# A second pair of heads' keys by seven products: context sums made earlier, weight pieces on POOL, nine warming products

## The chip, the cores and the metric

The kernel runs on one core of a Trainium2 chip. The metric is device time in microseconds (us) for one execution. A core has a matrix engine (PE; its weight loads are listed as PEld), a vector engine (DVE), a scalar engine (ACT), a general engine (POOL) and a queue engine (SP) that issues the DMA transfers here. Each runs its own list of instructions in order, and semaphores make one engine wait for another. Matmuls write to PSUM, a memory of eight banks; everything else lies in SBUF.

## What is computed

The reference is a gated cross-attention block followed by a gated feed-forward block. What matters here is the product of the context with the key weights, for 32 batches of 64 tokens (2048 tokens), 32 heads of 128, and a model width of 512:

```python
def _L0_xattn_ref(hidden_q, hidden_kv, attention_mask, position_bias, Wq, Wk, Wv, Wo):
    B, S, D, H, DH = (2, 128, 512, 32, 128)
    ...
    q = (hidden_q @ Wq).reshape(b, lq, h, dh)
    k = (hidden_kv @ Wk).reshape(b, lk, h, dh)
    v = (hidden_kv @ Wv).reshape(b, lk, h, dh)
    score = jnp.einsum('bqhd,bkhd->bhqk', q, k) * scale + position_bias
    ...
    return ctx @ Wo
...
x = x + jnp.tanh(g_xattn[0]) * _L0_xattn_ref(_layernorm(x, axis=-1), ctx_4096, mask_BxSxS2_bk0, fside_Bx32xSxS2_0, L0_xattn_Wq, L0_xattn_Wk, L0_xattn_Wv, L0_xattn_Wo)
x = x + jnp.tanh(g_ffn[0]) * _L0_ffn_ref(_layernorm(x, axis=-1), ...)
```

## The kernel before

**Stages.** The 2048 tokens are worked in two halves of 1024 (p = 0 and 1), the 32 heads in 16 pairs (n = 0 to 15). Each half makes the keys of all pairs (`stage_a`), then the values, then queries, scores, softmax and the output projection; the feed-forward block ends the program. Keys go to DRAM (`kd`) and come back later.

**Split numbers.** Matmuls are done on float32r values. To keep accuracy, each operand is split into a high half (an ACT cast to float32r, L90 or L296) and a low half (raw minus high, a subtraction on DVE or POOL, L91 or L300). One block product is three matmuls, high by high, high by low and low by high, for each of two pieces of 128 rows of the width: six matmuls, called passes here, of 128x128 by 128x512, all recorded at L100 in `mm3`.

**Blocks.** A pair's key product is seen as a product of 2 by 2 blocks. The context has b11, b21 (from the tile `f0`, the first 512 tokens), b12 and b22 (from `f1`); the pair's weights have a11, a12, a21, a22, each 128x256. It can be made in two ways:

- Plainly, by eight block products (`plain_half`, 48 passes), from the split blocks themselves. PSUM tiles are `ppk`, evicted by ACT at L400.
- By seven block products p1 to p7 (`unit`, 42 passes), from sums of blocks on both sides. `unit` makes p1, p6, p7, p5 and p2 and leaves p4 and p3 to a function `end`, which the next unit calls (`carry`) after its own p1. p2 is added into p1's PSUM tile `px`, p4 into p7's tile `pv`, p3 into p5's tile `pz`; so p2 waits until ACT has read `px` (L362), and p4 and p3 until DVE has added `pv` and `pz` to the result (L357).

For the seven products the context side needs p1 = b11, p2 = b21 and p3 = b22 and four sums (`sum_blocks`, L162): b12 - b11 (for p5, written over b11), `t2`, which is b22 minus that one (p6, tile `c0t` in the profile), b22 - b12 (p7, written over b12) and b21 - t2 (p4, written over b21). Each is two pieces of 128x512, subtracted and split on DVE, with casts on ACT. These are made once for a half and serve all pairs. On the weight side every pair has its own four sums s1 to s4 (L289, tile `wsk`) and seven splits (L296 on ACT, L300 on POOL, tiles `wk<pair>p<product>`).

**The first half's start.** `first_load` brings the weights of pair 0 and `f0`, then `f1`. While these come, 10 matmuls of the identity by itself keep PE busy (L520, tile `warm`; each shows as two passes). `first_blocks` then splits b11 (p1), b21 (p2), b12 (a plain block, `c0b`) and b22 (p3) as they land, makes the first matmuls of pair 0 directly from unsplit numbers (`very_first`, L408), and splits the four weight blocks of pair 1 with DVE (`prep_plain` with `weng`, which is `nc.vector`; tile `wk1a`), after which the raw weights of pair 3 are fetched into the buffer of pair 1's. Pairs 0 and 1 of this half are made plainly, and all later ones by seven products. In the second half all are made by seven products.

**What sets the order.** The order is written out by hand. Generators are put on the list `streams`, and each call of `beat` lets every generator go one step; the plain products have 8 beats a pair, a unit has 7. `sum_blocks` is a stream from pair 0 on (its last step is drained before pair 2). `key_blocks` is the stream of weight pieces on POOL and ACT: its loop over pairs takes seven steps a pair, in which it makes pair n's sums and pieces for p7, p6, p5 and p2, the p1 piece of pair n + 1, and the p4 and p3 pieces of pair n - 1; after the last of these it fetches the raw weights of pair n + 1 on SP. `wbp` has nine buffers for weight pieces, `kqp` two for finished keys, PSUM eight.

Of the kernel before, what the change touches and what calls it, by code (L numbers as in the profile page):

```python
# [43 lines left out]
def flamingo_block(ctx: ExitStack, tc: tile.TileContext, x, xT, ctxT, bias, mask, gx, gf,  # L44
# [17 lines left out]
    streams = []  # L62
# [93 lines left out]
    def sum_blocks(f, tags, nm, eng, out):  # L156
        b11, b21, b12, b22 = parts(f)
        t2 = [rows.tile([P, 512], F32, tag="row", name=f"{nm}t2_{kt}") for kt in range(2)]

        def sub(o, a, b):  # L160
            for kt in range(2):
                eng.tensor_tensor(o[kt], a[kt], b[kt], ALU.subtract)  # L162

        sub(b11, b12, b11)
        yield
        sub(b12, b22, b12)
        yield
        sub(t2, b22, b11)
        yield
        out["p6"] = act_block("p6", t2, tags, nm, eng)  # L170
        yield
        out["p7"] = act_block("p7", b12, tags, nm, eng)
        yield
        out["p5"] = act_block("p5", b11, tags, nm, eng)
        yield
        sub(b21, b21, t2)
        yield
        out["p4"] = act_block("p4", b21, tags, nm, eng)
# [79 lines left out]
    raw_of, wt = {}, {}  # L258
# [60 lines left out]
    def prep_plain(n, eng, only=None):  # L319
        raw = raw_of[("k", n)]  # L320
        out = wt.setdefault(("k", n), {})
        for i, a in enumerate(("a11", "a12", "a21", "a22")):
            if only is None or a in only:
                t = wbp.tile([P, 2, 256], F32R, tag="wb", name=f"wk{n}{a}")
                split(raw[:, i * 256:(i + 1) * 256], t[:, 0], t[:, 1], eng)
                out[a] = [(t[:, 0, kt * P:(kt + 1) * P], t[:, 1, kt * P:(kt + 1) * P]) for kt in range(2)]
# [104 lines left out]
    def first_blocks(p, f, tags, nm, weng, out, plain):  # L431
        g = p * NPR
        b11, b21, b12, b22 = parts(f)

        def block(q, raw, eng=nc.vector):
            t = big(tags[ORDER.index(q)], [P, 2, 2, 512], F32R, f"{nm}{q}")
            out[q] = []
            for kt in range(2):
                split(raw[kt], t[:, 0, kt], t[:, 1, kt], eng)
                out[q].append((t[:, 0, kt], t[:, 1, kt]))  # L440
                yield

        prep_plain(g, nc.gpsimd, ("a21",))
        yield from block("p1", b11, weng)
        prep_plain(g, nc.gpsimd, ("a22",))
        yield from block("p2", b21, weng)
        prep_plain(g, nc.gpsimd, ("a11", "a12"))
        plain.update({(1, 1): out["p1"], (2, 1): out["p2"]})
        plain["ps"] = very_first(raw_of.pop(("k", g)), wt["k", g], plain)
        yield  # L450
        fetch("k", g + 2, "r0")
        yield
        b12t = [rwp.tile([P, 2, 512], F32R, tag=f"r{2 + i}", name=f"{nm}b12{i}") for i in range(2)]
        plain[1, 2] = []
        for kt in range(2):
            split(b12[kt], b12t[0][:, kt], b12t[1][:, kt], nc.vector)
            plain[1, 2].append((b12t[0][:, kt], b12t[1][:, kt]))
            yield
        yield from block("p3", b22)
        plain[2, 2] = out["p3"]  # L460
        for a in ("a11", "a21", "a12", "a22"):
            prep_plain(g + 1, weng, (a,))
            yield
        raw_of.pop(("k", g + 1))
        fetch("k", g + 3, "r1")


    def next_blocks(f, tags, nm, out, gate):
# [47 lines left out]
    for _ in load_ctx(0, f, KT):  # L516
        pass
    warm = psum("warm")
    for i in range(10):
        nc.tensor.matmul(warm[:, :P], ident, ident, start=True, stop=True)  # L520
    fetch("k", 1, "r1")
    first = {}, {}
# [184 lines left out]
    def stage_a(p, first, fc, res, rot, more, enter, blocks):  # L707
        xc, plain = first
        f = None
        for n in range(NPR):  # L710
            g = p * NPR + n
            if n == 0 and plain:
                sums = sum_blocks(fc, res, f"c{p}", nc.vector, xc)
                streams.append(sums)
            if n == 0 and not plain:
                drain(blocks)
            if n == (1 if plain else 0):
                streams.append(key_blocks(p, n + 1))
            if n == 3:
                f = [big(f"f{j}", [P, KT, 512], F32, f"xf{p}_{j}") for j in range(2)]  # L720
                t7 = big(rot[7], [P, 2, 1024], F32, f"wvr{p}_0a")
                t8 = big(rot[8], [P, 2, 1024], F32, f"wvr{p}_0b")
                fetch_v(p, 0, [t7[:, 0], t7[:, 1], t8[:, 0], t8[:, 1]])
                if more:
                    more = paced(more, 2)
                    streams.append(more)
                xstat = x_stats(p)
                streams.append(xstat)
            if n == 5:
                vsum = [None] + [rwp.tile([P, 1024], F32, tag=f"r{2 + i}", name=f"vs{p}_0_{i}") for i in range(2)] + [None]  # L730
                v0 = paced(blocks_v(p, 0, rot, vsum, nc.vector, K_ORDER), 3)
                streams.append(v0)
            if 6 <= n < 6 + KT:
                for j in range(NCH):
                    nc.sync.dma_start(out=f[j][:, n - 6, :], in_=xT[p * NCH + j, n - 6])
            if n == 6 and p:
                drain(more)
                streams.append(acc_rstd(p - 1))
            if n == 10:
                drain(xstat)  # L740
                x_spread(p)
            if n == 10 and p:
                turned_acc = acc_turned(p - 1)
                streams.append(turned_acc)
            kt = k_tile(g)
            w = wt[("k", g)]

            def store(kt=kt, n=n):
                for i in range(2):
                    nc.sync.dma_start(out=kd[p][n][:, i, :], in_=kt[:, i, :])  # L750
            if n < 2 and plain:
                for j in range(2):
                    plain_half(w, plain, k_dst(kt), f"k{g}", j, plain["ps"] if n == 0 and j == 0 else None)
                store()
            else:
                if n == 2 and plain:
                    drain(sums)
                carry[:] = [unit(w, xc, None, k_dst(kt), f"k{g}", tuple(carry)), store]
        drain(v0)
        if p:  # L760
            drain(turned_acc)
        xnorm = paced(x_norm(p, f), 2)
        streams.append(xnorm)
        xq = {}
        for g in range(NG):
            if g == 2:
                drain(xnorm)
                streams.append(mask_stream(p))
                if p == 0:
                    streams.append(adapt)  # L770
            if g == NG - 1:
                t4 = pieces(rwp.tile([P, 1024], F32, tag="r1", name=f"x{p}t4"))
                fetch("q", p * NPR, "r0")
                bias = enter()
                streams.append(turned_blocks(f, [rot[(7 * NG + i) % 9] for i in range(7)], f"x{p}", nc.gpsimd, keep,
                                             t4, xq, bias, enter))
            for t in range(4):
                if t == 1:
                    if g + 1 < NG:
                        raw = [rwp.tile([P, 1024], F32, tag=f"r{i}", name=f"wvr{p}_{g + 1}_{i}") for i in range(4)]  # L780
                        fetch_v(p, g + 1, raw)
                        streams.append(blocks_v(p, g + 1, rot, None, nc.gpsimd, V_ORDER))
                    if g == NG - 2:
                        keep = {}
                        streams.append(turned_sums(f, f"x{p}", nc.gpsimd, keep))
                if t == 2 and g == NG - 1:
                    streams.append(prep("q", p * NPR, nc.gpsimd))
                vt = kqp.tile([P, 4, 512], F32, tag="kq", name=f"vt{p}_{g}_{t}")
                dst = {(i, j): vt[:, i * 2 + j, :] for i in range(2) for j in range(2)}
                after = unit(wt["v", p, g], xc, slice(t * P, (t + 1) * P), dst, f"v{p}_{g}_{t}", tuple(carry))  # L790

                def store(vt=vt, g=g, t=t):
                    for i in range(2):
                        for j in range(2):
                            nc.sync.dma_start(out=vd[p][2 * g + i][:, j * 4 + t, :], in_=vt[:, i * 2 + j, :])
                carry[:] = [after, store]
        enter()
        return xq
# [541 lines left out]
    for p in range(NPH):  # L1340
        qt = [rot[(7 * NG + i) % 9] for i in range(7)]
        rest = [t for t in rot if t not in qt]
        g = (p + 1) * NPR
# [118 lines left out]
```

## Time and profile before

| | us |
|---|---|
| three runs | 1519.61, 1519.88, 1520.21 |
| median | 1519.88 |
| profiled execution | 1520.39 |
| its span, first to last instruction | 1518.6 |
| granted TensorE clock, mean | 1.000 |

In the timeline a line has the start and the length in us, the engine, the source line, the operation, the tile written and those read, the shape, the number of instructions merged into the line, and in brackets the idle time ahead of them and what ended it. `c` is raw context, `c0p` a split context block or sum for a product, `c0b` the split plain block b12, `c0t` the sum t2, `rawk` raw key weights. Pair 0's plain products run from 5.77 to 17.55 us, pair 1's from 17.55 to 28.43, and pair 2's unit begins there. Most lines are short, so the table of costliest groups on the page has none of the first 30 us; the timeline of these has to be asked for by itself.

| stretch, us | DVE busy | ACT busy | POOL busy |
|---|---|---|---|
| 12 to 24.3 | 12.13 | 8.12 | 0.00 |
| 30 to 60 | 14.77 | 12.21 | 26.12 |

### The profile page before, as it was taken

The page shows a single profiled execution, that of the slowest core. Times are in us where ns is not written, and L with a number is a line of the kernel's source. Part 1 is how long each engine was busy: PE and PEld are TensorE (multiplying, and loading weights), DVE is VectorE, ACT ScalarE, POOL GpSimd, SP SyncE. Part 2 cuts the span into 40 slices and gives each one's busy share as a digit, 9 for nine tenths or more (in the row PEclk, how much of TensorE's full clock was granted, in tenths as well). Part 3 has the DMA queues.
Part 4 walks back from the last instruction along what each step waited for, and adds up shares of the span by engine and source line. Part 5 has one row for each costly group of instructions (what it writes and reads, how often), then busy time and mean ns, then how long its engine had stood idle before and what let it go on. Part 6 is the DMA issues. An engine that isn't in the chain of part 4 may idle for free.

```text
span 1518.6 us, 25096 instructions
## 1 busy us (share of the span) xinstructions
PE 1513.4 (100%) x8956; PEld 1278.3 (84%) x8956; DVE 941.6 (62%) x1587; ACT 717.7 (47%) x1582; POOL 1051.1 (69%) x1160
## 2 busy tenths in 40 slices
PE   9999999999999999999999999999999999999998
PEld 7888888888888888888888888888888888888887
DVE  5665554376677576666388755437666757666664
ACT  5444133355654664576344423335565466456511
POOL 4899378978675757668789947897867565766410
PEclk9999999999999999999999999999999999999999
DMA  5754554385335263442485664438533526444421
GB/s 206 279 195 153 188 178 167 138 280 186 129 132 184 89 221 140 149 144 76 159 290 204 235 208 176 167 138 287 179 131 128 186 90 219 143 154 132 112 70 70
DMA packets 130271, 254.79 MB, mean 168 GB/s; under 512 B 27393, under 2 KB 61185, under 8 KB 126050
## 3 DMA queue, kind: packets, MB, share of 16 engines
q1 hardware_dynamic: 129858, 252.67, 48.1%
q8 instruction: 70, 1.15, 0.3%
q10 hardware_dynamic: 288, 0.52, 0.1%
q14 instruction: 55, 0.45, 0.1%
HBM read 177.64 MB, written 75.51 MB: 167 GB/s over the span
## 4 chain that ended last, share of the span: by engine, by line
PE 100%; POOL 0%; DVE 0%; DVEq 0%; issue 0%; POOLq 0%
PE pa L100 23%; PE po L1015 8%; PE pxq L100 6%; PE pvq L100 6%; PE pzv L100 6%; PE pvv L100 6%; PE pxv L100 6%; PE pzq L100 6%; PE pzk L100 5%; PE pvk L100 5%; PE pxk L100 5%; PE ps L868 4%; PE pf L100 3%; PE pyq L100 3%; PE pyv L100 3%; PE pyk L100 3%
## 5 line engine op out<-in xcount | busy, mean ns | idle before, releaser
L100 PE MATMUL pa<-wo,ch 128*128 128x512 f32 x896 | 278.1, 391 | 0.0
L903 ACT COPY pt<-tp 32x256 f32<-32x256 f32 x452 | 182.4, 404 | 60.1 <-DVE tp L906 49.6
L100 PEld LDWEIGHTS pa<-wo,ch 128*128 128x128 f32 x896 | 166.8, 188 | 34.9
L100 PE MATMUL pa<-wo,cl 128*128 128x512 f32 x448 | 174.5, 390 | 0.0
L1064 DVE TENSOR_TENSOR acc<-pa,acc 128x512 f32<-128x512 f32 x192 | 129.9, 682 | 55.7 <-PE pa L100 55.7
L821 POOL TENSOR_TENSOR sm<-sm,madd 128x512 f32<-128x512 f32 x60 | 77.0, 1292 | 88.5 <-DMA sm<-bias 88.5
L895 POOL TENSOR_TENSOR sm<-sm,r 128x512 f32<-128x512 f32 x64 | 66.8, 1044 | 74.7 <-DVE r L894 74.0
L1015 PEld LDWEIGHTS po<-pt,v 128*128 128x128 f32 x960 | 111.6, 192 | 2.2
L1015 PE MATMUL po<-pt,v 128*128 128x128 f32 x960 | 112.5, 275 | 0.0
L873 POOL TENSOR_TENSOR sm<-sm,mx 128x512 f32<-128x512 f32 x64 | 67.0, 1048 | 62.1 <-DVE mx L872 62.1
L357 DVE TENSOR_TENSOR vt<-pvv,vt 128x512 f32<-128x512 f32 x64 | 44.1, 689 | 100.5 <-PE pvv L100 100.5
L1020 DVE TENSOR_TENSOR cl<-po,ch 128x512 fp32r<-128x512 f32 x112 | 76.5, 691 | 38.9 <-ACT ch L1019 38.6
L100 PEld LDWEIGHTS pa<-wo,cl 128*128 128x128 f32 x448 | 84.1, 188 | 17.8
L1019 ACT CAST ch<-po 128x512 fp32r<-128x512 f32 x112 | 65.9, 590 | 50.2 <-PE po L1015 48.3
L357 DVE TENSOR_TENSOR qT<-pvq,qT 128x512 f32<-128x512 f32 x64 | 44.1, 690 | 73.3 <-PE pvq L100 73.2
L91 POOL TENSOR_TENSOR wo<-rawo,wo 128x512 fp32r<-128x512 f32 x56 | 71.0, 1290 | 15.2 <-ACT wo L90 15.2
L379 ACT COPY vt<-pxv 128x512 f32<-128x512 f32 x32 | 18.9, 589 | 131.0 <-PE pxv L100 131.0
L357 DVE TENSOR_TENSOR kT<-pvk,kT 128x512 f32<-128x512 f32 x60 | 41.1, 685 | 59.6 <-PE pvk L100 59.3
L882 ACT ACTIVATE sm<-sm 128x512 f32<-128x512 f32 x62 | 39.3, 633 | 79.7 <-POOL sm L873 79.7
L357 DVE TENSOR_TENSOR qT<-pzq,qT 128x512 f32<-128x512 f32 x64 | 44.2, 690 | 37.9 <-PE pzq L100 37.6
L193 POOL TENSOR_TENSOR vs<-wvr,wvr 128x512 f32<-128x512 f32 x24 | 31.8, 1334 | 48.3 <-DMA wvr<-wv 48.3
L357 DVE TENSOR_TENSOR vt<-pzv,vt 128x512 f32<-128x512 f32 x64 | 44.2, 691 | 33.1 <-PE pzv L100 32.4
(1004 smaller groups left out, 3926.1 us busy)
## 6 DMA issues: line engine op xcount, KB each, us to landing
kd<-kT SPq DMA_DIRECT2D x64, 512.0 KB, 3.8
vd<-vt SPq DMA_DIRECT2D x128, 256.0 KB, 2.4
kB<-kd SPq DMA_DIRECT2D x32, 1024.0 KB, 10.3
v<-vd SPq DMA_DIRECT2D x32, 1024.0 KB, 8.0
rawq<-wq SPq DMA_DIRECT2D x32, 512.0 KB, 3.3
sm<-bias SPq DMA_DIRECT2D x64, 256.0 KB, 4.4
rawo<-wo SPq DMA_DIRECT2D x32, 512.0 KB, 3.4
rawk<-wk SPq DMA_DIRECT2D x31, 512.0 KB, 5.3
```

The costliest lines, as they stand in the source:

```text
L91: eng.tensor_tensor(lo, raw, hi.bitcast(F32), ALU.subtract)
L100: nc.tensor.matmul(ps, a, b, start=start and i == 0, stop=stop and i == len(todo) - 1, skip_group_check=True)
L357: nc.vector.tensor_tensor(o, ps, i, ALU.add)
L821: nc.gpsimd.tensor_tensor(t, t, masks[p][0], ALU.add)
L868: nc.tensor.matmul(ps[h * S:(h + 1) * S, t, :], qT[:, i, tok], kT[:, i, tok], start=True, stop=True)
L873: nc.gpsimd.tensor_tensor(s, s, mx.unsqueeze(2).to_broadcast([P, NT, S]), ALU.subtract)
L895: nc.gpsimd.tensor_tensor(t, t, r.unsqueeze(2).to_broadcast([P, NT, S]), ALU.mult)
L903: f(pts[n == NPR - 2][dst, i, :, src], of[src, :, ki * 32:(ki + 1) * 32])
L1015: nc.tensor.matmul(ps[:, t * P:(t + 1) * P], b["v", n][:, c * 4 + t, i * P:(i + 1) * P], pts[n == NPR - 2][:, i, c * 4 + t, :], start=True ...
L1019: nc.scalar.copy(h[:, i, sl], ps)
L1020: nc.vector.tensor_tensor(lo[:, i, sl], ps, h[:, i, sl].bitcast(F32), ALU.subtract)
L1064: nc.vector.tensor_tensor(acc[t], ps, acc[t], ALU.add)
```

## The change

Pair 1 of the first half is made by seven products and no longer plainly. For this, `first_blocks` no longer splits pair 1's plain weight blocks on DVE, nor fetches pair 3's raw weights; the weight stream `key_blocks` starts with pair 1 in both halves, from pair 0's first beat on, so that pair 1's sums and low halves are made by POOL, and pair 3's raw weights are fetched by it. `sum_blocks` makes t2 ahead of b22 - b12, and pauses for three beats in place of one ahead of the sum for p4. Nine warming matmuls are issued in place of ten.

```diff
@@ sum_blocks
         sub(b11, b12, b11)
         yield
+        sub(t2, b22, b11)
+        yield
         sub(b12, b22, b12)
         yield
-        sub(t2, b22, b11)
-        yield
         out["p6"] = act_block("p6", t2, tags, nm, eng)
         yield
         out["p7"] = act_block("p7", b12, tags, nm, eng)
         yield
         out["p5"] = act_block("p5", b11, tags, nm, eng)
-        yield
+        for _ in range(3):
+            yield
         sub(b21, b21, t2)
         yield
         out["p4"] = act_block("p4", b21, tags, nm, eng)
@@ first_blocks
         plain[2, 2] = out["p3"]
-        for a in ("a11", "a21", "a12", "a22"):
-            prep_plain(g + 1, weng, (a,))
-            yield
-        raw_of.pop(("k", g + 1))
-        fetch("k", g + 3, "r1")
@@ flamingo_block
     warm = psum("warm")
-    for i in range(10):
+    for i in range(9):
         nc.tensor.matmul(warm[:, :P], ident, ident, start=True, stop=True)
@@ stage_a
             if n == 0 and not plain:
                 drain(blocks)
-            if n == (1 if plain else 0):
-                streams.append(key_blocks(p, n + 1))
+            if n == 0:
+                streams.append(key_blocks(p, 1))
@@ stage_a
-            if n < 2 and plain:
+            if n == 0 and plain:
                 for j in range(2):
                     plain_half(w, plain, k_dst(kt), f"k{g}", j, plain["ps"] if n == 0 and j == 0 else None)
                 store()
```

## The prediction

> **What bounds the kernel now.** I read the page's totals and its chain of waits first, to know which engine sets the end; then the sums by stretch, for how full the others are where the change works; then the timeline of the first 40 us.
>
> ```profile
> span 1518.6 us, 25096 instructions
> ...
> PE 1513.4 (100%) x8956; PEld 1278.3 (84%) x8956; DVE 941.6 (62%) x1587; ACT 717.7 (47%) x1582; POOL 1051.1 (69%) x1160
> ...
> PE 100%; POOL 0%; DVE 0%; DVEq 0%; issue 0%; POOLq 0%
> ```
>
> PE is busy from start to end and the chain runs through PE alone. So a matmul pass less is time saved, and a hole in PE is time lost: nothing later takes either back.
>
> ```profile
> 12.00:24.30 12.30, 12.30 (x56) 10.18 (x55) 12.13 (x23) 8.12 (x18) 0.00 (x0) 1.00 0.42 150
> ...
> 720.00:880.00 160.00, 160.00 (x708) 132.53 (x707) 111.80 (x205) 63.27 (x154) 135.91 (x173) 1.00 0.64 223
> ```
>
> The columns are the stretch, its length, busy time of PE, PE's weight loads, DVE, ACT and POOL, the granted clock, DMA share and GB/s. While pairs 0 and 1 are made DVE is full (12.13 of 12.30 us) and POOL does nothing at all. The change puts work on POOL exactly here, and leaves most of DVE's.
>
> ```profile
> 1.34 4.64 PE L520 MATMUL warm<-ident 128*128 128x128 f32 x20 [1.34 <-POOL ident masks.py:199]
> 5.77 2.00 PE L408 MATMUL ppk<-c,rawk 128*128 128x512 f32 x4
> ...
> 6.31 0.19 PEld L408 LDWEIGHTS ppk<-c,rawk 128*128 128x128 f32 x1 [0.24 <-issue]
> 6.74 0.19 PEld L408 LDWEIGHTS ppk<-c,rawk 128*128 128x128 f32 x1 [0.24 <-issue]
> ...
> 12.10 1.28 DVE L91 TENSOR_TENSOR c0p<-c,c0p 128x512 fp32r<-128x512 f32 x2
> ...
> 13.30 1.42 DVE L91 TENSOR_TENSOR wk1a<-rawk,wk1a 128x256 fp32r<-128x256 f32 x4
> ...
> 17.55 5.60 PE L100 MATMUL ppk<-c0p,wk1a 128*128 128x512 f32 x24
> ...
> 22.99 2.88 PE L100 MATMUL ppk<-c0b,wk1a 128*128 128x512 f32 x12
> ...
> 24.36 0.94 POOL L300 TENSOR_TENSOR wk2p<-rawk,wk2p 128x256 fp32r<-128x256 f32 x1 [12.74 <-ACT wk2p L296]
> ...
> 28.43 1.52 PE L100 MATMUL pxk<-c0p,wk2p 128*128 128x512 f32 x6
> 29.79 1.52 PE L100 MATMUL pyk<-c0p,wk2p 128*128 128x512 f32 x6
> ```
>
> Pair 1 runs from 17.55 to 28.43, 48 passes in 10.88 us, 0.2267 us a pass. One of the seven products is 6 passes, 1.36 us, as the step from 28.43 to 29.79 shows.
>
> **What it removes.** Pair 1 goes from 48 to 42 passes: 10.88 - 9.52 = 1.36 us. The seventh product's end and two more lie behind pair 2's first one, which changes their order and not their number.
>
> One warming product is two of the 20 warm passes, which start 0.21 us apart near the end (three of them take 0.85 us, one 0.42): 0.43 us. Its cover is real: the two transfers that the first key matmul waits for are issued at 0.71 and 0.72 us and take 3.4 and 3.6 us, so they are there by 4.3, and the matmul starts at 5.77 only because the warm passes end there. But its first pass takes 0.54 us (5.77 to 6.31) and the next 0.43 (6.31 to 6.74): PE is still slow until about 5.99, if slow is half speed (0.11 us lost is half of 0.22). Starting 0.43 earlier, in the slow part, gains half, 0.21. If the speed came up with the start it would be 0.43; if it comes with a number of passes, two key passes more run slow and lose 0.86, a loss of 0.43. I take 0.21, as if the moment stood still. The granted clock is 1.00 in these rows and doesn't show the slow part.
>
> The Trainium skill ("TensorE: Matmul & The Clock Gate", Part 1) says that the clock rises after a window of about 3.4 us of activity, counted in time and not in matmuls, with a phase that varies. By it the moment stays where it is, the term is 0.21 and the loss of 0.43 falls away; no run here shows the rule itself.
>
> **What it adds on DVE and POOL, the part that decides.** DVE loses four 128x256 subtractions (1.42 us). Its context work stays, four sums and four low halves of two pieces each: 16 subtractions of 128x512 behind the two low halves of p3, 0.60 us apart (two take 1.28, one 0.68). But what was needed when pair 2 started (28.43 and later) is now needed by pair 1, from 18.7 us. POOL gets pair 1's weights: seven low halves and four sums of 128x256, 0.74 us each, 0.70 apart, where it stood idle, and pair 2's follow at once.
>
> Work them out with each engine alone first. PE starts pair 1 at 17.55 - 0.21 = 17.34; the next products are at 18.70 (p6), 20.06 (p7), 21.42 (p5), 22.78 (p2), 24.14 (pair 2's p1) and 25.50 (p4). p4 is added into PSUM tile pv, so it waits until DVE has read pv (add at L357), and that add stands in DVE's queue behind everything: from 12.70, 17 subtractions (17 x 0.60 = 10.25) and the adds of py and pv (0.60 + 0.69) end at 24.24. That is in time by 1.26 us. p6's low half would end at 18.2, p7's at 19.4, p5's at 20.6: all in time.
>
> But the two engines don't run alone:
>
> ```profile
> 9.34 2.29 POOL L91 TENSOR_TENSOR wk0a<-rawk,wk0a 128x256 fp32r<-128x256 f32 x2 [0.60 <-ACT wk0a L90]
> ...
> 10.12 2.05 DVE L91 TENSOR_TENSOR c0b<-c,c0b 128x512 fp32r<-128x512 f32 x2 [0.24 <-ACT c0b L90]
> ...
> 54.54 0.67 DVE L193 TENSOR_TENSOR vs<-wvr_0a,wvr_0b 128x512 f32<-128x512 f32 x1
> ...
> 54.61 1.20 POOL L300 TENSOR_TENSOR wk5p<-wsk,wk5p 128x256 fp32r<-128x256 f32 x1
> ...
> 119.75 0.69 DVE L357 TENSOR_TENSOR kT<-pzk,kT 128x512 f32<-128x512 f32 x1 [0.67 <-PE pzk L100]
> ...
> 120.36 0.73 POOL L289 TENSOR_TENSOR wsk<-rawk,wsk 128x256 f32<-128x256 f32 x1
> 120.36 1.28 DVE L193 TENSOR_TENSOR wvr_0a<-wvr_0a,vs 128x512 f32<-128x512 f32 x1
> ```
>
> At 54.54 DVE subtracts two SBUF tiles until 55.21; POOL's subtraction, begun at 54.61, ends at 55.81 and not at 55.35: 0.60 after DVE's. At 120.36 it is the other way: POOL ends at 121.09, DVE at 121.64, 0.55 later, where alone it takes 0.68. So while one works the other stands, and then pays 0.60 (POOL) or 0.55 (DVE). DVE's add of a PSUM tile (119.75) keeps its 0.69 beside POOL. In the rows at 9.34 and 10.12 the two alternate: two POOL and two DVE operations with nothing between take 1.15 us a pair. All 17 subtractions are of two SBUF tiles.
>
> By the order in which the changed program's instructions stand, POOL has an operation waiting nearly throughout: pair 1's first low half is free at 12.66 (its raw weights land at 12.16, ACT casts until 12.58), and it then has 11 operations of pair 1 and those of pair 2. It pauses only around 18.0 to 19.6, because ACT's cast of the p6 weight stands behind the two casts of p6's context block, and these wait for DVE; the two subtractions of b12 run free there, and one low half of p4 later, while POOL waits for ACT. So 14 of DVE's 17 pay both: 12.78 + 14 x 1.15 + 3 x 0.60 + 0.60 + 0.69 = 31.97. PE follows 0.06 later (as the first warm load follows ident): p4 starts at 32.0 in place of 25.50, 6.5 us late.
>
> On the way PE waits at p6 (its second low half ends near 22.1), p7 (24.4) and p5 (26.6), but that path alone would bring it to p4 at 30.1, so the wait for pv comes last and covers it. After it nothing is late: pz is read at 32.5 and p3 needs it at 33.4; POOL ends pair 2's p6 weight near 32.6, needed at 34.8.
>
> **What else is moved.** Pair 3's raw weights are fetched from the weight stream, once pair 1's last low half is read (near 27.3), behind pair 0's two stores on SP, and not right at the start. Landing 3.1 to 5.3 us later they are there by 32.6; their first cast stands on ACT behind pair 2's first eviction near 33.5. Zero; if they came a microsecond later, two weight casts of pair 2 behind them still have over 3 us. From here on weights are made 6 steps ahead of their unit, not 8. The second half of the tokens does it 5 ahead, and PE is busy 160.00 of 160.00 us there. Zero.
>
> **Sum.** -1.36 - 0.21 + 6.5 = +4.9 us. The profiled execution took 1520.39 us (span 1518.6 and 1.8 around it), 0.5 above the median of 1519.88, so 1524.8 by the median. Bounds of the collision: if only half of the 14 pay (each costs 0.55 over running alone), 3.8 less, sum +1.1; if all 17 pay, 1.6 more, sum +6.5.
>
> **Rivals.** (a) No collision that matters: POOL's operations slip into gaps, DVE keeps its pace, -1.57, 1518.3 us. For it: the margin of 1.26 us with each engine alone. Against it: DVE is full in this stretch, and every overlap of this kind that I looked at shows the delay. It decides up to 5 colliding operations: 1.26 of margin and 1.57 of gain, over 0.55 each. Not slower than before; 0.10. (b) The engines collide, but DVE gets more than every second turn, so that PE's own path decides, 30.1 and earlier: +1 to +3, 1522 us; five operations in a row that alternate are the longest series in the trace; 0.13. (c) The collision, and PE falls back to slow speed in its holes (the longest about 2 us), and needs again what it needed at the start, 1.34 to 5.99: half of 4.65 lost, 2.3 more, 1527.1 us. No hole in this trace tells. 0.12. That pair 1 isn't made by seven products at all is excluded: the built program has 42 passes there.
>
> The page on TensorE says that the clock falls after an idle window of about 3.4 us. My longest hole is shorter, so by the page +4.9 stands and (c) doesn't come.
>
> **How the numbers follow.** The forecast has 0.65; it gives 1524.8, by its own bounds (three collisions fewer, three more) 1523 to 1526.5. The range reaches to most of (b) and to (c): 1521.5 to 1528. Over 0.2% (3.0 us, about what a measurement can tell from no change) means above 1522.9: nearly all of the forecast, (c), and a quarter of (b): 0.79. (a) and the rest of (b) lie within it: 0.20. Faster by 0.2% would need 3 us, and all that is removed is 1.8: 0.01.
>
> **What would show it.** Right: between 12.7 and 31 us DVE's subtractions last near 1.2 us and POOL's too; PE has holes ahead of p6, p7, p5 and the largest, about 2 us, ahead of pair 1's p4; after 35 us none. Pair 0's first matmul starts near 5.34. Wrong: subtractions of 0.68 beside a busy POOL, or PE without a hole from 17 to 35 us, which is (a).

## The result, and the profile after

The changed kernel takes 1525.36 us (median of six runs, 1525.23 to 1526.88); the kernel before beside it took 1519.82 (six runs, 1519.54 to 1520.70). The ratio is 1.0035, 95% interval 1.0025 to 1.0046: about 5.5 us slower. Forecast were 1524.8 and a loss of 4.9.

The page of the changed kernel, its totals:

```profile
span 1525.1 us, 25099 instructions
...
PE 1515.8 (99%) x8948; PEld 1278.5 (84%) x8948; DVE 953.0 (62%) x1588; ACT 718.2 (47%) x1583; POOL 1064.4 (70%) x1171
```

PE issues eight passes less (8948 for 8956: six of one product and two of one warming product) and the span is 6.5 us longer. The totals don't say where. The sums by stretch of the changed kernel do; the columns are those of before (stretch, length, PE, PEld, DVE, ACT, POOL, granted clock, DMA share, GB/s):

```profile
12.00:24.30 12.30, 10.03 (x39) 7.24 (x39) 12.30 (x14) 8.06 (x18) 10.71 (x10) 0.93 0.18 60
...
17.30:30.00 12.70, 10.42 (x36) 7.07 (x34) 12.70 (x14) 8.06 (x19) 11.16 (x11) 0.87 0.33 124
30.00:36.30 6.30, 4.45 (x13) 3.53 (x14) 3.09 (x4) 2.64 (x8) 6.30 (x9) 0.73 0.01 3
36.30:60.00 23.70, 23.70 (x106) 19.63 (x105) 11.71 (x20) 8.15 (x20) 18.61 (x27) 1.00 0.82 297
```

From 12 to 24.3 us DVE is full (12.30 us; before 12.13) but has 14 instructions in this stretch where it had 23; POOL is busy 10.71 us where it stood idle. PE has lost its full rows, and the granted clock has fallen to means of 0.87 and 0.73. A finer division shows where:

```profile
22.50:25.90 3.40, 3.40 (x10) 2.28 (x9) 3.40 (x4) 2.34 (x6) 3.35 (x4) 0.50 0.62 252
25.90:32.70 6.80, 4.95 (x22) 3.65 (x21) 6.49 (x8) 2.84 (x7) 6.20 (x8) 1.00 0.30 105
32.73:36.14 3.41, 3.41 (x10) 2.63 (x9) 0.69 (x1) 1.59 (x5) 3.41 (x6) 0.50 0.02 5
```

The clock is at half in two stretches of 3.4 us and full between them. From 36.3 us on PE is full and the clock is 1.00 again.

The timelines of PE and of DVE in the changed kernel (start, length, and in brackets the idle time and what ended it):

```profile
17.05 1.52 PE L100 MATMUL pxk<-c0p,wk1p 128*128 128x512 f32 x6
18.86 0.51 PE L100 MATMUL pyk<-c0p,wk1p 128*128 128x512 f32 x1 [0.29 <-ACT wk1p L297]
21.35 1.56 PE L100 MATMUL pyk<-c0p,wk1p 128*128 128x512 f32 x5 [1.99 <-DVE c0p L91]
22.71 2.90 PE L100 MATMUL pvk<-c0p,wk1p 128*128 128x512 f32 x6
25.40 1.86 PE L100 MATMUL pzk<-c0p,wk1p 128*128 128x512 f32 x6
...
28.48 1.52 PE L100 MATMUL pxk<-c0p,wk2p 128*128 128x512 f32 x6
31.85 2.15 PE L100 MATMUL pvk<-c0p,wk1p 128*128 128x512 f32 x6 [1.85 <-DVE kT L358]
33.80 2.63 PE L100 MATMUL pzk<-c0p,wk1p 128*128 128x512 f32 x6
36.26 1.54 PE L100 MATMUL pyk<-c0p,wk2p 128*128 128x512 f32 x6
```

```profile
11.98 1.28 DVE L91 TENSOR_TENSOR c0p<-c,c0p 128x512 fp32r<-128x512 f32 x2
13.19 2.37 DVE L162 TENSOR_TENSOR c<-c,c 128x512 f32<-128x512 f32 x2
15.48 2.37 DVE L162 TENSOR_TENSOR c0t<-c,c 128x512 f32<-128x512 f32 x2
17.77 2.39 DVE L162 TENSOR_TENSOR c<-c 128x512 f32<-128x512 f32 x2
20.09 1.81 DVE L91 TENSOR_TENSOR c0p<-c0t,c0p 128x512 fp32r<-128x512 f32 x2
21.82 4.66 DVE L91 TENSOR_TENSOR c0p<-c,c0p 128x512 fp32r<-128x512 f32 x4
26.40 2.37 DVE L162 TENSOR_TENSOR c<-c,c0t 128x512 f32<-128x512 f32 x2
28.69 0.68 DVE L358 TENSOR_TENSOR kT<-pyk,kT 128x512 f32<-128x512 f32 x1
29.29 1.81 DVE L91 TENSOR_TENSOR c0p<-c,c0p 128x512 fp32r<-128x512 f32 x2
31.02 0.68 DVE L358 TENSOR_TENSOR kT<-pvk,kT 128x512 f32<-128x512 f32 x1
```

Two subtractions take 1.28 us alone, 2.37 with POOL in both, 1.81 with POOL in one: by this measure 14 of the 17 from 12.6 us on collided. Adds of a PSUM tile keep 0.68. The last row is the add that frees pv. It ends at 31.70, and PE's p4, which waits for it, starts at 31.85 us.

The account for the two profiled executions: before, pair 1 starts at 17.55 and pair 2's second product at 29.79; after, at 17.05 and 36.26. So the start is 0.50 us earlier; one product less is 1.36; p4 starts at 31.85 and not six products after 17.05, at 25.21, which is 6.64 lost; and p4 with p3 take 4.41 us in place of 2.72, which is 1.69 lost, in the second stretch at half clock. -0.50 - 1.36 + 6.64 + 1.69 = +6.47, all that the span grew by (1525.1 - 1518.6 = 6.5). The other five executions have spans of 1523.5 to 1523.7 at a granted clock of 0.999 to 1.000 where the profiled one has 1525.1 at 0.998. So slow passes explain the last 1.5 us of this one execution, and not the loss that all six share.

The first and the third term of this account hang together. p4 starts when DVE has read pv, so a pair 1 that starts earlier only waits longer. The spans agree: those of the kernel before scatter over 1.6 us (1517.8 to 1519.4 in all the runs beside the experiments), the five of the changed kernel over 0.2.

### The profile page after: what moved, and what is told of

It is laid out like the page before. It is cut to its first block, busy times and chain, and to the rows that moved or that the text cites. A ratio compares the mean times of both kernels' runs of the same rounds, so it can differ in the third digit from the quotient of the medians.

```text
span 1525.1 us, 25099 instructions
## 1 busy us (share of the span) xinstructions
PE 1515.8 (99%) x8948; PEld 1278.5 (84%) x8948; DVE 953.0 (62%) x1588; ACT 718.2 (47%) x1583; POOL 1064.4 (70%) x1171
## 3 DMA queue, kind: packets, MB, share of 16 engines
q8 instruction: 70, 1.15, 0.3%
## 4 chain that ended last, share of the span: by engine, by line
PE 98%; DVE 1%; DMA 0%; ACT 0%; issue 0%; SPq 0%; DVEq 0%
PE pa L100 23%; PE po L1011 8%; PE pxq L100 6%; PE pvq L100 6%; PE pzv L100 6%; PE pvv L100 6%; PE pxv L100 6%; PE pzq L100 6%; PE pzk L100 6%; PE pvk L100 5%; PE pxk L100 5%; PE ps L864 4%; PE pf L100 3%; PE pyq L100 3%; PE pyv L100 3%; PE pyk L100 3%
```

## The experiments

The theory: DVE's subtractions of two SBUF tiles and POOL's subtractions take turns, so that DVE's list ends late. Rivals: the operands are late by the order of the lists alone; the weights on POOL are late by themselves; the clock.

**POOL busy, but reading nothing.**

```diff
@@ pair_blocks, do: the sums
+                    if kind == "k" and n in (1, 2):
+                        for _ in range(2):
+                            nc.gpsimd.memset({"s1": s1, "s2": s2, "s3": s3, "s4": s4}[q], 0.0)
+                        continue
@@ pair_blocks, do: the low halves
+                    if kind == "k" and n in (1, 2):
+                        for _ in range(2):
+                            nc.gpsimd.memset(t[:, 1].bitcast(F32), 0.0)
+                        continue
```

> Leaves out POOL's subtractions and sums for the key weights of pairs 1 and 2 of the first half: each is replaced by two memsets of the tile that it would write, so that POOL stays about as busy but reads no SBUF. Collision of DVE and POOL: DVE's subtractions go back to 0.68 us each, PE has no hole over 0.3 us between 17 and 36 us, 1517.9 to 1518.3 us. Rival, that the operands are late by the order of the DVE and ACT lists alone: the holes ahead of p6, p7, p5 and p4 stay, 1523 us or more. If POOL's writing alone holds DVE up as well, also 1523 or more, with DVE at about 1.2 us.

Measured 1518.5 us (1518.11 to 1519.50; before beside it 1520.31; ratio 0.9990, 0.9981 to 0.9999), 0.2 above the range expected. DVE in this kernel:

```profile
13.30 1.28 DVE L162 TENSOR_TENSOR c<-c,c 128x512 f32<-128x512 f32 x2
14.50 1.28 DVE L162 TENSOR_TENSOR c0t<-c,c 128x512 f32<-128x512 f32 x2
15.71 1.28 DVE L162 TENSOR_TENSOR c<-c 128x512 f32<-128x512 f32 x2
16.91 1.28 DVE L91 TENSOR_TENSOR c0p<-c0t,c0p 128x512 fp32r<-128x512 f32 x2
18.12 2.49 DVE L91 TENSOR_TENSOR c0p<-c,c0p 128x512 fp32r<-128x512 f32 x4
...
23.58 0.68 DVE L366 TENSOR_TENSOR kT<-pvk,kT 128x512 f32<-128x512 f32 x1
```

And its sums by stretch:

```profile
12.00:24.30 12.30, 12.30 (x55) 10.02 (x54) 12.27 (x21) 10.04 (x23) 8.67 (x31) 1.00 0.42 138
17.00:35.00 18.00, 18.00 (x81) 14.91 (x80) 11.42 (x18) 11.48 (x29) 14.01 (x36) 1.00 0.56 186
```

With POOL busy 8.67 us of 12.3 every subtraction is back at 0.68, pv is read at 24.3 (worked out in the prediction for each engine alone: 24.24), PE is full and the clock stays at 1.00. DVE's list, its order and its amount are the same, so order alone isn't the cause. The sums that other engines wait for come sooner as well here, but that can't shorten a DVE operation. The Trainium skill ("SBUF — State Buffer", Who interferes with whom) says that a DVE instruction with two SBUF inputs contends with a GpSimd instruction that reads SBUF and not with one that only writes it; these rows agree.

**Whose pieces.** The same memsets for one pair only, pair 1 (no_read_1, shown) or pair 2 (no_read_2, with `(2,)`).

```diff
-    if kind == "k" and n in (1, 2):
+    if kind == "k" and n in (1,):
```

> Leaves out POOL's sums and low halves for pair 1's key weights only (two memsets each); pair 2's are made. Collision, counted by operations of POOL that meet DVE's subtractions before the add that frees pv: three of pair 2 are left (1.6 us), of which 1.3 us of slack takes most: 1518.3 to 1519.5 us. Rival, that pair 2's pieces crowd POOL and DVE: 1522 or more.

> Leaves out POOL's sums and low halves for pair 2's key weights only (two memsets each); pair 1's are made. Collision: the changed kernel less four or five operations of POOL of 0.55 us each ahead of the add that frees pv, 1522.5 to 1523.3 us; the largest hole, ahead of pair 1's p4, shrinks from 2.4 to under 0.5 us. Rival, that pair 1's weights decide alone: as the changed kernel, 1525.4.

Measured 1519.0 us (1518.21 to 1519.59) and 1523.73 (1523.55 to 1523.84), before beside them 1520.13. Pair 2's pieces alone cost nothing: in no_read_1 PE is full (18.00 of 18.00 us from 17 to 35). Of the three pieces that I had counted, only one falls among DVE's subtractions, and there it is POOL that waits:

```profile
20.40 2.10 POOL L309 TENSOR_TENSOR wk2p<-rawk,wk2p 128x256 fp32r<-128x256 f32 x1 [3.07 <-ACT wk2p L301]
20.62 1.28 DVE L162 TENSOR_TENSOR c<-c,c0t 128x512 f32<-128x512 f32 x2
```

DVE makes two subtractions at its own pace while POOL's one takes 2.10 us, so the turns do not alternate in every case. On top of pair 1's pieces those of pair 2 cost: without them, in no_read_2, p4 starts 0.56 us after the pass ahead of it and not 2.24. The time is 0.4 above what I expected; p6's hole stays as it was (1.99 us in both).

**The same operations with one operand in PSUM.**

```diff
-    t2 = [rows.tile([P, 512], F32, tag="row", name=f"{nm}t2_{kt}") for kt in range(2)]
+    t2 = [psum(f"{nm}t2_{kt}") for kt in range(2)]
```

> The changed kernel with the sum t2 (two pieces) held in PSUM and not in SBUF; same operations, order and data. The four subtractions that read t2 (p6's two low halves and the two of b21) then have one SBUF input each. Collision of two SBUF inputs: in the profile these four take about 0.7 us beside a busy POOL and not 1.2, the add that frees pv comes up to 4 x 0.55 = 2.2 us earlier, 1523 to 1524 us. Rival, that any DVE operation is held up while POOL works: they keep 1.2 us, 1525.4.

Measured 1523.35 us (1522.86 to 1523.47; before 1520.11; ratio 1.0020, 1.0011 to 1.0029). DVE in this kernel:

```profile
19.01 1.22 DVE L162 TENSOR_TENSOR c<-c 128x512 f32<-128x512 f32 x1
20.15 1.27 DVE L91 TENSOR_TENSOR c0p<-c0t,c0p 128x512 fp32r<-128x512 f32 x2
21.35 4.10 DVE L91 TENSOR_TENSOR c0p<-c,c0p 128x512 fp32r<-128x512 f32 x4
25.37 1.27 DVE L162 TENSOR_TENSOR c<-c,c0t 128x512 f32<-128x512 f32 x2
```

The rows at 20.15 and 25.37 are the four subtractions that read t2: 1.27 us for two, where the changed kernel had 1.81 and 2.37 (three of the four had collided), between neighbours that still collide (1.22 alone, and three of the four at 21.35). The add that frees pv starts at 29.18 and not at 31.02. The edit changes nothing else, and POOL is as busy as in the changed kernel (16.38 of 18 us from 17 to 35; there 16.46). This tells the theory from "DVE is slow beside a busy POOL" most cleanly. The granted clock is 1.00 from 6 to 60 us in this profile, so the 3.2 us that are left of the loss aren't the clock's either.

**Pair 1's pieces on DVE.**

```diff
-    prev, nxt = none, pair_blocks("k", p * NPR + n0, nc.gpsimd)
+    prev, nxt = none, pair_blocks("k", p * NPR + n0, nc.gpsimd if p else nc.vector)
```

> The changed kernel with pair 1's sums and low halves made by DVE and not by POOL. If what counts is the turns on a common path to SBUF, an operation of 128x256 costs DVE 0.34 us by itself and 0.55 us as POOL's turn: pair 1's eleven cost 3.7 in place of about 5.5, pair 2's on POOL still collide, 1523 to 1524.5 us. Rival, that work belongs on the engine that is idle: slower than the changed kernel, 1526 or more.

Measured 1525.20 us (1525.14 to 1525.95): as the changed kernel, and 0.7 above my range. DVE and PE in this kernel:

```profile
19.48 1.29 DVE L91 TENSOR_TENSOR c0p<-c0t,c0p 128x512 fp32r<-128x512 f32 x2 [1.48 <-ACT c0p L90]
20.69 0.42 DVE L290 TENSOR_TENSOR wsk<-rawk,wsk 128x256 f32<-128x256 f32 x1
21.02 0.42 DVE L301 TENSOR_TENSOR wk1p<-wsk,wk1p 128x256 fp32r<-128x256 f32 x1
22.10 1.29 DVE L91 TENSOR_TENSOR c0p<-c,c0p 128x512 fp32r<-128x512 f32 x2 [0.66 <-ACT c0p L90]
...
31.16 0.68 DVE L358 TENSOR_TENSOR kT<-pvk,kT 128x512 f32<-128x512 f32 x1
```

```profile
21.60 1.08 PE L100 MATMUL pyk<-c0p,wk1p 128*128 128x512 f32 x2 [3.07 <-ACT wk1p L297]
24.12 2.07 PE L100 MATMUL pyk<-c0p,wk1p 128*128 128x512 f32 x4 [1.44 <-DVE wk1p L301]
...
32.67 1.52 PE L100 MATMUL pvk<-c0p,wk1p 128*128 128x512 f32 x6
```

The collisions are gone but for one, and the price of a piece on DVE was right (0.33 us from the piece at 20.69 to the next). What I had left out is that DVE then stands still behind the casts of its own context blocks on ACT (1.48 and twice 0.66 us), and that pair 1's pieces stand in its list behind these waits. So pv is read at 31.16 all the same. But p4 doesn't wait for it here: it starts at 32.67, right behind the product ahead of it. The time is lost earlier, at p6, which waits 3.07 us for the cast of its weights and 1.44 for their low half, and in slow passes behind it (granted clock 0.50 from 21.8 to 28.6 us). Even without its waits DVE's 17 subtractions, 11 pieces and two adds are 10.25 + 11 x 0.34 + 1.29 = 15.3 us from 13.0 on, to 28.3, some 3 us past the time at which p4 is due: an estimate, but it suggests that moving the pieces can't save this form.

**The order of the sums.**

```diff
-    sub(t2, b22, b11)
-    yield
     sub(b12, b22, b12)
     yield
+    sub(t2, b22, b11)
+    yield
 ...
-    for _ in range(3):
-        yield
+    yield
     sub(b21, b21, t2)
```

> The changed kernel with the old order of the sums (t2 after b22 - b12) and one beat ahead of the sum for p4. As many operations collide, so the end of DVE's list hardly moves; p6 has to wait two operations longer and ACT's casts for p4 come ahead of the eviction of px: 1525.4 to 1527 us. Rival, that this order decides whether the operands are in time: 1528 or more.

Measured 1526.80 us (1525.02 to 1527.80). The time lies in the range expected and excludes the rival, but not by the way expected. In the profiled execution (1527.79) only 10 of the 17 subtractions are stretched, and the add that frees pv starts at 29.69 and not at 31.02. The largest hole, 2.45 us, is now ahead of p2, which waits for the eviction of px, and behind it the granted clock is 0.50 from 28 to 34.8 us. Two of the five executions take 1525.0 us, 0.3 less than the changed kernel. So the order moves the holes, and no loss or gain by the order itself is shown.

**The weights on POOL, without the seven products.**

```diff
-    prep_plain(g + 1, weng, (a,))
+    prep_plain(g + 1, nc.gpsimd, (a,))
```

> The kernel before, with the four low halves of pair 1's plain weights made by POOL and not by DVE. Collision: four operations of POOL of 0.60 us alternate with four of DVE between 12.6 and 17.5 us, but eight plain products need no context sum before pair 2 and PE needs these weights from 17.55 on: 1519.8, within 0.3 us of before. Rival, that weights of pair 1 on POOL are late by themselves: a hole in PE after 17.5 us, 1521 or more.

Measured 1520.17 us (1519.92 to 1521.02; before 1520.31; ratio 1.0001, 0.9992 to 1.0009). Four of DVE's subtractions are stretched to 1.2 us between 12.7 and 17.3 us, and PE is held up only at 29.8 us, by 0.2. Collisions cost only where DVE's list is the one that is due.

**The warming products.** `range(10)` in the changed kernel; `range(9)` and `range(8)` in the kernel before.

```diff
-    for i in range(10):
+    for i in range(9):
```

> The changed kernel with ten warming products again. The warming term alone: the first key matmul starts 0.43 us later; the profiles of before and after put the whole term at 0.50 us, my prediction at 0.21. Expected 1525.6 to 1525.9 us against 1525.4. If the clock comes up after a number of passes and not after a time, 1525.0 or less.

> The kernel before with nine warming products and nothing else changed. Expected 0.2 to 0.5 us faster than before, 1519.3 to 1519.6. If the clock comes up after a number of passes, 0.4 slower, 1520.2.

> The kernel before with eight warming products. The profiles so far show the clock coming up between 4.1 and 6.3 us, another time in each execution, so the term is between 0.4 and 0.85 us for executions in which it comes early, and about half of that where it comes late: 1519.2 to 1519.7 against 1520.1, hardly told from no change. If it is under 0.2 us, what starts earlier waits for its data.

Measured 1526.79 us (1525.35 to 1527.11), 1520.20 (ratio 1.0001, 0.9992 to 1.0010) and 1519.59 (ratio 0.9997, 0.9988 to 1.0005). The first two miss what was expected, the third lies in its range, and none is told from its partner. The second equals the 1520.2 named for a fixed number of passes, but the kernel before took 1520.31 beside it, so nine products aren't slower. The traces say why. In the changed kernel the start of pair 1 decides nothing. With ten products it starts at 17.30 us and not 17.05, but p4, which waits for DVE, starts at 31.83 where it started at 31.85:

```profile
31.83 2.08 PE L100 MATMUL pvk<-c0p,wk1p 128*128 128x512 f32 x6 [1.81 <-DVE kT L358]
```

The median with ten products is higher because three of its five executions, and one of six with nine, have a span of 1525.0 to 1525.3; the slow passes there are the subject of the next experiment. In the kernel before the start does count, but it isn't constant. The weight loads at the start of PE, in before and in no_read_12:

```profile
4.92 0.76 PEld L520 LDWEIGHTS warm<-ident 128*128 128x128 f32 x3
5.56 0.51 PEld L408 LDWEIGHTS ppk<-c,rawk 128*128 128x128 f32 x2
6.31 0.19 PEld L408 LDWEIGHTS ppk<-c,rawk 128*128 128x128 f32 x1 [0.24 <-issue]
```

```profile
4.68 0.30 PEld L417 LDWEIGHTS ppk<-c,rawk 128*128 128x128 f32 x2
```

A load that takes 0.19 us at full speed is slow until about 6 us in the one and fast by 4.7 in the other, which has one warming product fewer. In the thirteen profiles of this study the first fast load comes between 4.2 and 7.7 us, in no order of the number of warming products. A fixed number of passes isn't the rule either: in kernels with nine products 14 (no_read_12) to 22 loads (old_order) come ahead of it. This moves the start of pair 1 by more than one product is worth: with nine products it lies between 16.67 us (no_read_12) and 18.09 (old_order).

**The clock in the holes.** Eight products of the identity are put into the largest hole.

```diff
+    def filler():
+        fill = psum("fill")
+        for i in range(8):
+            nc.tensor.matmul(fill[:, :P], ident, ident, start=True, stop=True)
     carry[:] = [unit(...), store]
+    if n == 1 and plain:
+        carry.insert(0, filler)
```

> The changed kernel with eight products of the identity put into the largest hole of PE, ahead of pair 1's p4 (1.8 us at full speed in a hole of 2.4). In the profile of the changed kernel the passes after that hole stand 0.427 us apart until 36.3 us and not 0.227, and its executions lie at 1525.3 or at 1526.8. If the idle time lets the clock fall, these passes come back to 0.227, and all executions lie near 1525.3, with none at 1526.8. Rival, that the slow passes have another cause: both levels stay; if the filler itself is late, 1526 or more.

Measured 1525.48 us (1525.16 to 1526.80). Its PE:

```profile
29.97 1.95 PE L757 MATMUL fill<-ident 128*128 128x128 f32 x16
31.98 1.63 PE L100 MATMUL pvk<-c0p,wk1p 128*128 128x512 f32 x6
33.44 1.53 PE L100 MATMUL pzk<-c0p,wk1p 128*128 128x512 f32 x6
34.81 1.52 PE L100 MATMUL pyk<-c0p,wk2p 128*128 128x512 f32 x6
```

p3 takes 1.53 us and not 2.63, pair 2's p6 starts at 34.81 and not 36.26, the granted clock from 30 to 35 us is 1.00, and the span is 1523.6 and not 1525.1. So in this profile the slow passes are gone with the idle time. Other profiles fit: where the same hole is short (0.17 us in no_read_2, 0.99 in t2_psum) p4 and p3 run at full speed, and where it is long (1.81 in seven_w10) they don't. That the idle time is the cause isn't shown by this, since five of the six executions of the changed kernel have spans of 1523.5 to 1523.7 without these products.

What I expected of the executions held for the spans and not for the times. All five spans are 1523.4 to 1523.7, none is at 1525. The times go up to 1526.80 all the same, since these executions take 1.8 to 3.1 us beside their span, where those of all other kernels here take 1.7 to 1.9. Where this extra comes from stays open.

No kernel here that computes the whole beats the kernel before by more than its interval.

## Why the prediction was right

- **PE sets the end, and what is lost isn't taken back.** Shown: after 36.3 us the two traces run alike, and the account of the first 36 us gives the whole difference.
- **One product less, 1.36 us.** Shown: with POOL's reads gone (no_read_12), pair 2's second product starts 10.88 us after pair 1's first (16.67 to 27.55), and in the kernel before 12.24 (17.55 to 29.79). The kernel is 1.8 us faster.
- **Each engine alone would be in time.** Shown by the same run: pv read at 24.3.
- **14 of 17 subtractions collide, p4 at 32.0.** Measured 14, and 31.85. Which three escape was partly wrong for this execution: one of p4, as predicted, but also the last low half of p3 and the second of p6, and not the two of b12, since POOL's pauses were shorter (0.43 us ahead of the p6 piece, where I had 1.6). In the profiles of seven_w10 and filled 14 collide too, and the three that escape are those predicted. The count matters and not the names.
- **The cause is two SBUF inputs beside POOL's reads.** Shown from both sides, by taking POOL's reads away (no_read_12) and by taking one of DVE's inputs to PSUM (t2_psum).
- **The fetch of pair 3's weights and the shorter lead, zero.** PE has no hole after 36.3 us.
- **The warming product, 0.21.** Mis-sized, and without effect. The two profiles have 0.50, and the moment at which PE comes to full speed differs between executions by more than 3 us: "as if the moment stood still" was the wrong picture. It did no harm, since p4's start is set by DVE: counted without the term, p4 would be due at 25.71, its 32.0 be 6.29 late, and the sum the same.
- **Rival (c), slow speed in the holes, 2.3 more.** It came, in part: 1.69 us in the profiled execution (granted clock 0.50 from 32.73 to 36.14 us), while the spans of the other five are 1.4 to 1.6 us shorter. I had set it at 0.12 and let the Trainium skill ("TensorE: Matmul & The Clock Gate", Part 1) speak against it, which has the clock fall after an idle window of about 3.4 us. Here the longest hole is 2.0 us, and the clock fell; the measurement decides.
- **Rival (a)** fell: it would need that POOL's pieces meet at most five of DVE's subtractions. **Rival (b)** fell: seven of DVE's subtractions in a row, from 13.19 to 20.09 us, start 1.15 us apart. That DVE can get more than every second turn does occur (no_read_1, at 20.40), but not where it would have helped.

The sum was 0.6 us below the median. Most of that seems to be what I took off for the median; this is an estimate. From the profiled 1520.39 us the sum gives 1525.3, close to the 1525.36 measured; I then took off 0.5, since the median of the kernel before is that much lower. But its executions seem to differ by their start: in the four profiles with a plain pair 1 the spans go from 1517.9 to 1518.6, and what follows the start of pair 1 is 1501.0 to 1501.2 in all of them. The changed kernel waits such a difference out ahead of p4. In its profiled execution the slow passes' 1.7 us, which I had left out, came on top.

## What to carry to other kernels

An engine that stands idle isn't yet a resource: before work is put on POOL beside DVE, look at what both read. Where both subtract SBUF tiles, their two lists were nearly one list here, and their times added. Count the operations that meet, at 0.55 us for a DVE operation of 128x512 here, and compare with the slack of the one result that PE waits for. A result that only DVE and ACT read can go to PSUM, which took the operations that read it out of the count here. And a gain ahead of such a wait is no gain: the earlier start of PE was lost again at p4.

## What was not expected of the hardware

- The granted clock fell to 0.50 for 3.4 us twice in a stretch in which PE waits in holes of at most 2.0 us (from 22.5 to 25.9 and from 32.73 to 36.14 us); passes then stand 0.427 us apart and not 0.227. With work of no use in the second hole it was 1.00 there.
- PE came to full speed at 4.2 to 7.7 us in thirteen profiled executions, though its first matmul starts at 1.34 us in all of them.
